# Edge items of a sparse graph layer in another order, with the last panels' own rows and the last features in tiles of their own

## The chip, the cores and the metric

One core of a Trainium2 chip runs the whole kernel. The metric is the time of one execution on the device in microseconds (us); of the kernel before, three executions took 3121.13 us (median), 3118.40 and 3138.08 us. One further execution was taken with the profiler on.

## The reference

The input x holds 32 graphs of 512 nodes with 256 features; one 512x512 adjacency matrix serves all. Four layers follow each other, of which the first and the last (called 0 and 3 in the names) have the same form:

```python
def _L0_gnn_ref(h_t, A_a, A_m, W1, b1, W2, b2, Wa, ba, Wm, bm, beta1, beta2, beta3):
    d = h_t.shape[-1]
    pre_u = jnp.einsum('bud,dk->buk', h_t, W1[:d])
    pre_v = jnp.einsum('bvd,dk->bvk', h_t, W1[d:])
    hidden = jax.nn.relu(pre_u[:, :, None, :] + pre_v[:, None, :, :] + b1)
    S = jax.nn.sigmoid(jnp.einsum('buvk,ko->buvo', hidden, W2)[..., 0] + b2[0])
    a_t = jnp.einsum('buv,bud->bvd', S * A_a, h_t)
    m_t = jnp.einsum('uv,bud->bvd', A_m, h_t) * h_t
    return (beta1 * h_t + beta2 * (jnp.einsum('bvd,de->bve', a_t, Wa) + ba)
            + beta3 * (jnp.einsum('bvd,de->bve', m_t, Wm) + bm))
...
    x = _L0_gnn_ref(x, adj, adj, ...)   # layer 0; A_a and A_m are both adj
    x = _L1_gnn_ref(x, adj, ...)        # z + relu((adj z) W' + b)
    x = _L2_gnn_ref(x, adj, ...)        # dense attention: softmax(leaky_relu(f_i + f_j) + adj) feats + x
    x = _L3_gnn_ref(x, adj, adj, ...)
```

Only some ten entries in a row of adj are not zero, so S is needed only there.

## The kernel before, in words

**Groups.** The 32 graphs go in eight groups of NB = 4, numbered t = 0 to 7. A group passes four streams of work: `first` (pre-activations of layer 0 into a table in memory), `edges` of layer 0 (the values of S at the edges), `middle` (the sums of layer 0, layers 1 and 2, the pre-activations of layer 3) and `edges` and `last` of layer 3. `sparse_path` gives every piece of every stream a due time in units of one group's middle stage, and `weave` issues the pieces in the order of these times, so that pieces of neighbouring groups alternate on each engine. Every engine executes its own instructions in the order in which they stand in its queue.

**Items.** An edge item is a set of 128 edges of the graph, one for each partition, handled for the four graphs of the group at once. Each of the four blocks of 128 nodes has OWN = 8 items (one edge per node and item); edges beyond eight per node go to PANELS = 2 panel items for each half of the node range. That makes ITEMS = 36 in a pass of `edges`, and there are 16 passes (two in each group). Blocks 0 and 1 and their panels form the first half of S, blocks 2 and 3 the second.

**One item.** `fetch` gathers the rows of the far ends (`rows`, 512 KB, an indirect DMA on GpSimd's queue, line 607) and needs the near ends' rows (`mine`): for a block's items these are one contiguous tile, loaded once by SyncE (line 647) and shared by its eight items; for a panel they are gathered by a second indirect DMA on GpSimd (also through line 607). There are three buffers for `mine`. VectorE adds the two (line 686), multiplies the positive part by W2 (line 694 or 702), ScalarE or VectorE sums, and after each four items a sigmoid follows (exp in line 592, then lines 596, 597 and 636). `put` then scatters the item's 128x4 values into memory (`cells`, an indirect DMA on GpSimd, line 601). There is one `cells` tensor for each half of S; two puts into the same tensor are kept apart by a wait for the earlier one to land. So `put` takes from the list `ready` the first entry that belongs to the other half than the put before it, if there is one. Rows are fetched LEAD = 3 items ahead; in the first pass of the kernel (layer 0, t = 0) and in the last (layer 3, t = 7) it is LEAD_AT_ENDS = 5, with some more tiles for rows (`rows_more`).

**S in use.** `load` reads the filled half tensors back as four tiles `SA` of 1 MB (line 727, GpSimd's queue); tiles 0 and 1 come from the first half, 2 and 3 from the second. In `middle` ScalarE copies one graph out of each (`flat`, line 809), and TensorE multiplies (line 840); in layer 3 TensorE reads SA itself (line 1001).

**The end.** For t = 7 the work of layer 3 that does not need S is done ahead by `last_before`: for each of four graphs it loads the features x2 (`h`, line 957, two buffers) and their transpose (`hT`, line 962, one buffer), and TensorE makes hWa and mhT from them (line 45; copies in lines 740 and 750) and keeps them in tiles `big`. `last_behind` then loads SA and does the sums (lines 1001, 1010, 1013) and the store (line 985).

**The order of the items** is a list made once for all passes; `h0` and `h1` below are the halves:

```python
order = [item_of(0, j) for j in range(OWN // 2)]
for lead, other in ((0, 2), (2, 1), (1, 3)):
    for j in range(OWN // 2):
        order += [item_of(lead, OWN // 2 + j), item_of(other, j)]
tail = [panel_of(h, q) for h in range(2) for q in range(PANELS)]
for j in range(OWN // 2):
    order.append(item_of(3, OWN // 2 + j))
    order += tail[j : j + 1]
```

By halves this reads 0000, then twelve pairs that alternate, then 1 0 1 0 1 1 1 1: the last eight are block 3's second four items with the panels h0, h0, h1, h1 between them.

Of the kernel before, what the change touches and what calls it, by code (L numbers as in the profile page):

```python
# [8 lines left out]
F32 = mybir.dt.float32  # L9
# [7 lines left out]
P = 128  # L17
N = 512
D = 256
NC = N // P  # L20
DC = D // P
# [7 lines left out]
OWN = 8  # L29
PANELS = 2  # L30
LINES = PANELS * P
LEAD = 3
LEAD_AT_ENDS = 5
TAIL = 6
CELLS = HALF * N
ITEMS = NC * OWN + 2 * PANELS
SPARE = NC // 2 * OWN * P + LINES
GROUP = NB * D
# [173 lines left out]
def item_of(c, k):  # L212
    return c * OWN + k


def panel_of(half, q):
    return NC * OWN + half * PANELS + q


class Edges:  # L220
# [3 lines left out]
    def __init__(self, m, pool):  # L224
        nc = self.nc = m.nc
        self.m = m
        self.iu = pool.tile([P, 2 * PANELS], I32, name="iu")
        self.iv, self.cell = (pool.tile([P, ITEMS], I32, name=n) for n in ("iv", "cell"))
        self.value = pool.tile([P, ITEMS], F32, name="value")
        self.inode = pool.tile([P, 2 * PANELS], I32, name="inode")  # L230

        order = [item_of(0, j) for j in range(OWN // 2)]
        for lead, other in ((0, 2), (2, 1), (1, 3)):
            for j in range(OWN // 2):
                order += [item_of(lead, OWN // 2 + j), item_of(other, j)]
        tail = [panel_of(h, q) for h in range(2) for q in range(PANELS)]
        for j in range(OWN // 2):
            order.append(item_of(3, OWN // 2 + j))
            order += tail[j : j + 1]
        self.order = order  # L240

    def value_of(self, j):
# [172 lines left out]
class Sparse:  # L415
# [192 lines left out]
            out=rows, out_offset=None, in_=g.table, in_offset=bass.IndirectOffsetOnAxis(ap=at, axis=0)  # L608
        )

    def edges(self, g, spare=()):

        nc, e, w = self.nc, self.e, g.w
        flat = "p c b -> p (c b)"
        own = g.self_s.rearrange(flat)
        ready, fetched = [], {}
        lead = LEAD_AT_ENDS if spare else LEAD
        tags = [None] * 5 + list(spare)  # L620
        mine = {}
        places = g.table.rearrange("(c p k) n -> c k p n", p=P, k=2)

        def own_1():
            self.sigmoid_of(own)
            diag = self.counts.diag.unsqueeze(2).to_broadcast([P, NC, NB])
            nc.vector.tensor_tensor(g.self_s, g.self_s, diag, ALU.mult)
            for q in range(2):
                diagonal = g.cells[q][q * HALF : q * HALF + HALF * (N + 1), :]
                diagonal = diagonal.rearrange("(c p a) b -> p c a b", p=P, a=N + 1)[:, :, 0, :]  # L630
                nc.sync.dma_start(diagonal, g.self_s[:, 2 * q : 2 * q + 2, :])

        def run_1(ks):
            self.sigmoid_of(g.s[:, ks, :].rearrange(flat))
            value = e.value[:, ks].unsqueeze(2).to_broadcast([P, ks.stop - ks.start, NB])
            nc.vector.tensor_tensor(g.s[:, ks, :], g.s[:, ks, :], value, ALU.mult)
            for k in range(ks.start, ks.stop):
                j = e.order[k]
                ready.append((e.half_of(j), e.cell[:, j : j + 1], g.s[:, k, :]))

        def fetch(n):
            j = e.order[n]
            c = j // OWN
            if c >= NC or c not in mine:
                t = self.gath.tile([P, GROUP], F32, name="mine", bufs=3)
                if c < NC:
                    nc.sync.dma_start(t, places[c, 0])
                    mine[c] = t
                else:
                    self.fetch(t, g, e.iu[:, j - NC * OWN : j - NC * OWN + 1])  # L650
            else:
                t = mine[c]
            if tag := tags[n % len(tags)]:
                rows = self.act.tile([P, GROUP], F32, name="rows_more", tag=tag)
            else:
                rows = self.gath.tile([P, GROUP], F32, name="rows")
            self.fetch(rows, g, e.iv[:, j : j + 1])
            fetched[n] = rows, t

        def put():  # L660

            at = next((n for n, r in enumerate(ready) if r[0] != self.half), 0)
            if ready:
                r = ready.pop(at)
                self.half = r[0]
                self.put(g, *r)

        def sums(k, rows):

            for b in range(NB):  # L670
                part = rows[:, b * D : (b + 1) * D]
                self.behind(nc.scalar.activation(part, part, AF.Identity, accum_out=g.s[:, k, b : b + 1]))  # L672

        summed = []
        self.half = 1
        for n in range(lead):
            fetch(n)
            yield

        todo = [(2, lambda: self.exp_of(w, own)), (4, own_1)]  # L680
        done = 0
        for k in range(ITEMS):
            for _ in range(2 if spare and len(ready) > 2 else 1):
                put()
            rows, other = fetched.pop(k)
            self.behind(nc.vector.tensor_tensor(rows, rows, other, ALU.add))  # L686
            if k + lead < ITEMS:
                fetch(k + lead)
            if summed:
                summed.pop(0)()  # L690
            if spare or k % 2 == 1 and k < ITEMS - 3:
                by_entry = rows.rearrange("p (b d) -> p b d", b=NB)
                w2 = w["W2bc"].unsqueeze(1).to_broadcast([P, NB, D])
                nc.vector.scalar_tensor_tensor(by_entry, by_entry, 0.0, w2, ALU.max, ALU.mult)  # L694
                summed.append(lambda k=k, rows=rows: sums(k, rows))
                if spare:
                    summed.pop(0)()
            else:
                for b in range(NB):
                    part = rows[:, b * D : (b + 1) * D]  # L700
                    at = g.s[:, k, b : b + 1]
                    nc.vector.scalar_tensor_tensor(part, part, 0.0, w["W2bc"], ALU.max, ALU.mult, accum_out=at)  # L702
            if k % 4 == 3 or k >= ITEMS - 3:
                ks = slice(done, k + 1)
                near = spare or k >= ITEMS - 5
                todo.append((k + (1 if near else 3), lambda ks=ks: self.exp_of(w, g.s[:, ks, :].rearrange(flat))))
                todo.append((k + (1 if near else 4), lambda ks=ks: run_1(ks)))
                done = k + 1
            while todo and todo[0][0] <= k:
                todo.pop(0)[1]()  # L710
            yield
        for _, f in todo:
            f()
        for _ in range(TAIL - 1):
            put()
            yield
        while ready:
            put()
        yield
# [237 lines left out]
        self.nc.sync.dma_start(h, self.x2s[i])  # L957
        return h

    def x2T_of(self, i):  # L960
        hT = self.act.tile([P, DC, N], F32, name="hT3", tag="hT")
        self.nc.sync.dma_start(hT, self.x2T[i])
        return hT

    def last_before(self, g, i):

        self.ends = []
        for b in range(NB):
            h, hT = self.x2_of(i + b), self.x2T_of(i + b)
            both = self.big(F32, 2048, 0).rearrange("p (k n) -> p k n", k=2)  # L970
            hWa = both[:, 0, :].rearrange("p (c d) -> p c d", c=NC)
            mhT = both[:, 1, :].rearrange("p (c n) -> p c n", c=DC)
            for _ in self.hWa(g, hT, 3, hWa):
                yield
            for _ in self.mhT(h, hT, 3, mhT):
                yield
            self.ends.append((hWa, mhT))
# [78 lines left out]
def edge_times(ahead, a, b, behind, lead=LEAD):  # L1056

    step = (b - a) / ITEMS
    first = [ahead + j * min(step, (a - ahead) / lead) for j in range(lead)]
    return first + spread(even(ITEMS), a, b) + spread(even(TAIL), b, behind)  # L1060
# [18 lines left out]
def sparse_path(ctx, m, counts, xr, outr, B):  # L1079


    sp = Sparse(ctx, m, counts, xr, outr, B)
    last = B // NB - 1
# [6 lines left out]
    for t in range(last + 1):  # L1090
        g0, g3 = Group(sp, m.g0, f"0_{t}"), Group(sp, m.g3, f"3_{t}")
# [11 lines left out]
        edges3 = edge_times(end + 0.003, end + 0.05, end + 0.48, end + 0.54)  # L1103
        behind = end + 0.56, end + 1.13
        if t == last - 1:
            edges3 = edge_times(end + 0.003, end + 0.05, end + 0.46, end + 0.5)
            behind = end + 0.7, end + 1.06
        if t == last:
            end -= 0.2
            edges3 = edge_times(end + 0.003, end + 0.02, end + 0.45, end + 0.46, LEAD_AT_ENDS)  # L1110
# [2 lines left out]
            (sp.first(g0, t * NB), first, "fill"),  # L1113
            (sp.edges(g0, ("yT", "mhT3") if t == 0 else ()), edges0, ""),
            (sp.middle(g0, g3, t * NB), spread(middle_shares(t == 0), start, end), "main"),
            (sp.edges(g3, ("yT", "h1", "hT1") if t == last else ()), edges3, "free"),
        ]
        if t == 0:
            streams.append((sp.middle_before(g0, 0), spread(AHEAD, -0.15, -0.03), ""))
# [243 lines left out]
```

## Time and profile before

| what | us |
|---|---|
| median of three executions | 3121.13 |
| the profiled execution | 3102.14 |
| its span | 3100.4 |
| TensorE busy in the span | 2714.6 |
| VectorE busy | 2302.8 |
| GpSimd busy | 1522.5 |
| first four S tiles (SA of layer 0, t = 0): first and last load issued at | 242.9 and 262.1 |
| last pass of edges: first row gather and last put issued at | 2885.6 and 3039.3 |
| last S tiles: last load issued at | 3042.5 |
| last matmul group begins at | 3092.2 |

Times inside the span are counted from its start. One period, from a group's SA loads to the next group's, lasts some 358 us (1872 to 2230). Busy times of a stretch of the profile (columns: stretch, length, busy us and count of each engine, mean granted TensorE clock, share of the DMA engines, GB/s moved):

```profile
1877.00:2235.00 358.00, 333.61 (x1072) 202.84 (x1071) 281.91 (x764) 155.44 (x464) 187.98 (x160) 0.97 0.71 229
2880.00:3100.40 220.40, 161.88 (x566) 123.36 (x564) 115.84 (x154) 70.95 (x315) 99.33 (x80) 0.88 0.55 185
```

The engines stand in the order TensorE matmul, TensorE weight load, VectorE, ScalarE, GpSimd. In a period in the midst of the kernel TensorE is busy for 334 of 358 us; in the last 220 us it is busy for 162.

### The profile page before, as it was taken

How to read it: one execution, taken by the hardware profiler on the slowest of the kernel's cores; microseconds unless marked ns; L12 is line 12 of the kernel's file. 1: busy time of each engine (PE TensorE's matmuls, PEld its weight loads, DVE VectorE, ACT ScalarE, POOL GpSimd, SP SyncE). 2: the span in 40 equal slices, each digit the busy share in tenths (PEclk: the TensorE clock that was granted, in tenths of full speed). 3: DMA queues.
4: the chain of work that ended last, by engine and by line, in shares of the span. 5: the costliest groups of instructions: out<-in, count | busy, mean ns of one | idle time of the engine just before them, and what ended most of it. 6: DMA issues, size and time to landing. Idle time of an engine off the chain costs nothing.

```text
span 3100.4 us, 32465 instructions
## 1 busy us (share of the span) xinstructions
PE 2714.6 (88%) x8645; PEld 1642.5 (53%) x8646; DVE 2302.8 (74%) x6026; ACT 1337.8 (43%) x4101; POOL 1522.5 (49%) x1312
## 2 busy tenths in 40 slices
PE   6366888889998999989998999989999899889957
PEld 3133444446654565546664565545664566545636
DVE  6783886889589875989589885888679795772761
ACT  3453554445345433545354442545335343453440
POOL 1462453556346563556346562565436563450561
PEclk9688988999999999999999999999999999999978
DMA  8874556786677766786668766787568766551753
GB/s 285 282 236 152 180 174 225 237 268 213 223 224 263 235 210 219 247 282 213 227 213 258 238 197 213 242 267 237 188 216 268 251 221 208 178 174 58 234 195 115
DMA packets 302719, 679.40 MB, mean 219 GB/s; under 512 B 52672, under 2 KB 170944, under 8 KB 294336
## 3 DMA queue, kind: packets, MB, share of 16 engines
q0 software_dynamic: 120384, 406.01, 41.0%
q1 hardware_dynamic: 163184, 234.01, 22.5%
q10 hardware_dynamic: 18960, 37.24, 3.2%
q8 instruction: 70, 1.15, 0.2%
q14 instruction: 121, 0.99, 0.1%
HBM read 531.12 MB, written 146.01 MB: 218 GB/s over the span
## 4 chain that ended last, share of the span: by engine, by line
PE 51%; DVE 18%; DMA 17%; issue 6%; ACT 4%; POOL 3%; SPq 0%; POOLq 0%; ACTq 0%; DVEq 0%
PE pst L45 24%; PE pst L1001 7%; DVE rows L686 6%; DMA table<-puv 5%; DMA rows<-table,iv 5%; PE pst L570 3%; DVE rows L702 3%; PE pst L861 3%; PE pst L1010 3%; PE pst L572 3%; DMA cells<-s,cell 3%; DVE rows L694 3%; PE pst L883 2%; PE pst L840 2%; DMA SA<-cells 2%
## 5 line engine op out<-in xcount | busy, mean ns | idle before, releaser
L601 POOL DMA_INDIRECT cells<-s,cell x576 | 691.1, 1200 | 740.7 <-DMA cells<-s,cell 370.3
L607 POOL DMA_INDIRECT rows<-table,iv x554 | 663.3, 1197 | 672.7 <-DMA table<-puv 148.1
L686 DVE TENSOR_TENSOR rows<-rows,mine 128x1024 f32<-128x1024 f32 x554 | 670.8, 1219 | 164.7 <-DMA rows<-table,iv 148.8
L672 ACT ACTIVATE rows<-rows 128x256 f32<-128x256 f32 x1096 | 442.9, 407 | 516.7 <-DVE rows L694 511.1
L45 PE MATMUL pst<-adj,h 128*128 128x512 f32 x1024 | 451.3, 592 | 0.3 <-PE pst L941 0.3
L702 DVE SCALAR_TENSOR_TENSOR rows<-rows,L_gnn_W2bc 128x256 f32<-128x256 f32 x1120 | 415.9, 419 | 1.8
L45 PE MATMUL pst<-L_gnn_Wa,hT 128*128 128x256 f32 x1024 | 264.3, 410 | 118.6 <-DMA hT<-xT 64.6
L694 DVE SCALAR_TENSOR_TENSOR rows<-rows,L_gnn_W2bc 128x1024 f32<-128x1024 f32 x274 | 332.3, 1216 | 0.3
L45 PEld LDWEIGHTS pst<-adj,h 128*128 128x128 f32 x1024 | 192.8, 190 | 222.4 <-issue 218.4
L45 PEld LDWEIGHTS pst<-L_gnn_Wa,hT 128*128 128x128 f32 x1024 | 207.7, 208 | 165.8 <-issue 53.1
L45 PE MATMUL pst<-eT,feats 128*128 128x512 f32 x512 | 231.5, 606 | 12.4 <-ACT eT L953 12.4
L45 PE MATMUL pst<-adjT,zW 128*128 128x512 f32 x512 | 227.8, 597 | 6.2 <-ACT zW L865 6.2
L1001 PEld LDWEIGHTS pst<-hWa,SA 128*128 128x128 f32 x896 | 213.7, 328 | 7.7 <-issue 4.5
L1001 PE MATMUL pst<-hWa,SA 128*128 128x256 f32 x896 | 216.8, 398 | 0.0
L861 PE MATMUL pst<-WT,hT 128*128 128x256 f32 x512 | 150.3, 459 | 75.9 <-DVE hT L848 75.9
L672 ACT ACTIVATION_READ_ACCUMULATOR rows<-rows 128x1 f32 x1096 | 206.7, 189 | 0.0
L809 ACT COPY flat<-SA 128x512 f32<-128x512 f32 x128 | 137.6, 1128 | 155.0 <-PE pst L45 60.1
L840 PE MATMUL pst<-flat,hWa 128*128 128x512 f32 x448 | 196.8, 592 | 0.0
L861 PEld LDWEIGHTS pst<-WT,hT 128*128 128x128 f32 x512 | 118.0, 235 | 114.9 <-DVE hT L848 88.1
L575 ACT COPY puv<-pst 128x256 f32<-128x256 f32 x256 | 93.7, 370 | 183.8 <-DVE puv L574 168.1
L574 DVE TENSOR_TENSOR puv<-pst,bc_L_gnn_b 128x256 f32<-128x256 f32 x256 | 105.0, 416 | 90.3 <-DMA table<-puv 53.8
L45 PEld LDWEIGHTS pst<-eT,feats 128*128 128x128 f32 x512 | 97.5, 193 | 127.5 <-issue 109.8
(170 smaller groups left out, 3979.3 us busy)
## 6 DMA issues: line engine op xcount, KB each, us to landing
table<-puv SPq DMA_DIRECT2D x256, 256.0 KB, 5.5
SA<-cells POOLq DMA_DIRECT2D x64, 1024.0 KB, 7.0
h<-in_x_dram SPq DMA_DIRECT2D x64, 512.0 KB, 6.4
mine<-table SPq DMA_DIRECT2D x64, 512.0 KB, 5.3
hT<-xT SPq DMA_DIRECT2D x36, 512.0 KB, 5.1
h<-x2s SPq DMA_DIRECT2D x36, 512.0 KB, 4.1
xT<-hT ACTq DMA_DIRECT2D x32, 512.0 KB, 5.5
x2T<-yT SPq DMA_DIRECT2D x32, 512.0 KB, 5.3
```

Of the source, the lines that this page charges most:

```text
L45: nc.tensor.matmul(out, lhsT, rhs, start=(n == 0), stop=(n == len(pairs) - 1))
L574: nc.vector.tensor_tensor(puv[:, 0, :], pp[:, 0:D], w["b1bc"], ALU.add)
L601: self.nc.gpsimd.indirect_dma_start(out=g.cells[half], out_offset=bass.IndirectOffsetOnAxis(ap=at, axis=0), in_=s, in_offset=None)
L607: self.nc.gpsimd.indirect_dma_start(out=rows, out_offset=None, in_=g.table, in_offset=bass.IndirectOffsetOnAxis(ap=at, axis=0))
L672: self.behind(nc.scalar.activation(part, part, AF.Identity, accum_out=g.s[:, k, b : b + 1]))
L686: self.behind(nc.vector.tensor_tensor(rows, rows, other, ALU.add))
L694: nc.vector.scalar_tensor_tensor(by_entry, by_entry, 0.0, w2, ALU.max, ALU.mult)
L702: nc.vector.scalar_tensor_tensor(part, part, 0.0, w["W2bc"], ALU.max, ALU.mult, accum_out=at)
L809: self.nc.scalar.copy(flat[:, r, :], SA[r][:, :, b])
L840: nc.tensor.matmul(pz, hWa[:, r, cs], flat[:, r, :], start=(r == 0), stop=False)
L861: nc.tensor.matmul(pw[:, at], zT[:, d, cs], m.WT_1[:, d, :], start=(d + k == 0), stop=(d * k == 1))
L1001: nc.tensor.matmul(pz[:, k * D : (k + 1) * D], SA[r][:, cs, b], hWa[:, r, :], start=(r + k == 0), stop=False)
```

## The change

It has three parts. The list of items gets another order, for all 16 passes: blocks 0 and 2 run together up to the end of block 2, then blocks 1 and 3; the panels of the second half come in between, at places 20 and 27, and those of the first half at places 33 and 35. By halves: 0 0, then 16 that alternate, then 0 1 1 0 1 0 1 0 1 1 0 1 0 1 (places 18 to 31), then 1 0 1 0. In the last pass alone, the four panels' own rows are gathered after the first few items into tiles `held`, whose memory belonged to `eT`, `hWa0` and `mhT0` of the middle stage. And in `last_before` the transposed features of the second to fourth graph get a tile of their own each, in the memory of the S tiles of layer 3.

```diff
-        order = [item_of(0, j) for j in range(OWN // 2)]
-        for lead, other in ((0, 2), (2, 1), (1, 3)):
-            for j in range(OWN // 2):
-                order += [item_of(lead, OWN // 2 + j), item_of(other, j)]
-        tail = [panel_of(h, q) for h in range(2) for q in range(PANELS)]
-        for j in range(OWN // 2):
-            order.append(item_of(3, OWN // 2 + j))
-            order += tail[j : j + 1]
+        ends, most = OWN // 4, OWN - OWN // 4
+        order = [item_of(0, j) for j in range(ends)]
+        for j in range(most):
+            order += [item_of(0, ends + j), item_of(2, j)]
+        for j in range(ends):
+            order += [item_of(1, j), item_of(2, most + j)]
+        for j in range(most):
+            order += [item_of(1, ends + j), item_of(3, j)]
+            if j % (most // PANELS) == 0:
+                order.append(panel_of(1, j // (most // PANELS)))
+        for j in range(ends):
+            order += [item_of(3, most + j), panel_of(0, j)]
...
-    def edges(self, g, spare=()):
+    def edges(self, g, spare=(), panels=()):
...
-            if c >= NC or c not in mine:
+            if j in held:
+                t = held.pop(j)
+            elif c >= NC or c not in mine:
...
+        def hold():
+
+            js = [j for j in e.order if j >= NC * OWN]
+            for tag in panels:
+                n = 2 if tag == "eT" else 1
+                t = self.act.tile([P, n, GROUP], F32, name="held", tag=tag)
+                for k in range(n):
+                    j = js.pop(0)
+                    held[j] = t[:, k, :]
+                    self.fetch(held[j], g, e.iu[:, j - NC * OWN : j - NC * OWN + 1])
...
         for k in range(ITEMS):
             for _ in range(2 if spare and len(ready) > 2 else 1):
                 put()
+            if k == LEAD_AT_ENDS:
+                hold()
...
-    def x2T_of(self, i):
-        hT = self.act.tile([P, DC, N], F32, name="hT3", tag="hT")
+    def x2T_of(self, i, hT=None):
+        if hT is None:
+            hT = self.act.tile([P, DC, N], F32, name="hT3", tag="hT")
...
-            h, hT = self.x2_of(i + b), self.x2T_of(i + b)
+            room = self.big(F32, 2048, 3)[:, 0 : DC * N].rearrange("p (c n) -> p c n", c=DC) if b else None
+            h, hT = self.x2_of(i + b), self.x2T_of(i + b, room)
...
-            (sp.edges(g3, ("yT", "h1", "hT1") if t == last else ()), edges3, "free"),
+            (sp.edges(g3, *((("yT", "h1", "hT1"), ("eT", "hWa0", "mhT0")) if t == last else ())), edges3, "free"),
```

More of the change, by code (lines that the diff above doesn't have):

```diff
@@ L230, in __init__ @@
         self.inode = pool.tile([P, 2 * PANELS], I32, name="inode")
-        order = [item_of(0, j) for j in range(OWN // 2)]
-        for lead, other in ((0, 2), (2, 1), (1, 3)):
-            for j in range(OWN // 2):
-                order += [item_of(lead, OWN // 2 + j), item_of(other, j)]
-        tail = [panel_of(h, q) for h in range(2) for q in range(PANELS)]
-        for j in range(OWN // 2):
-            order.append(item_of(3, OWN // 2 + j))
-            order += tail[j : j + 1]
+        ends, most = OWN // 4, OWN - OWN // 4
[10 more added lines that the diff above has]
+            order += [item_of(3, most + j), panel_of(0, j)]
+        assert len(order) == len(set(order)) == ITEMS
         self.order = order
@@ L620, in edges @@
         tags = [None] * 5 + list(spare)
-        mine = {}
+        mine, held = {}, {}
         places = g.table.rearrange("(c p k) n -> c k p n", p=P, k=2)
```

## The prediction

> **What bounds the kernel now.** I read the page's busy slices first, then the chain of waits in order of time, then the timelines of GpSimd, VectorE and TensorE at the places where the chain leaves TensorE. TensorE is busy for 88% of the span and for 334 of 358 us in a period of the middle, so there an order of items can win little. The two ends are different: in the last 220 us it is busy for 162. The end of the chain of waits (start us, us, what):
>
> ```profile
> 2985.86 5.36 DMA rows_more<-table,iv
> 3004.48 8.06 DMA mine<-table,iu
> 3024.31 4.51 DMA hT<-x2T
> 3028.96 12.12 PE pst L45 x32
> 3042.54 8.43 DMA SA<-cells
> 3051.02 8.57 PE pst L1001 x26
> ```
>
> It runs from row gathers to a panel's own rows, to a feature load that had to wait for its only buffer, and then to the S tiles. From 3051.0 on nothing but TensorE's sums remains (35.8 of the 40 us from 3060 are busy), so the span ends 49.4 us after the last S tile is there. GpSimd's timeline shows what holds that tile (start, us, engine, line, what, idle before and its releaser):
>
> ```profile
> 3002.94 1.24 POOL L607 DMA_INDIRECT rows<-table,iv  x1 [0.30 <-issue]
> 3004.48 0.94 POOL L607 DMA_INDIRECT mine<-table,iu  x1 [0.30 <-issue]
> 3005.72 0.94 POOL L607 DMA_INDIRECT mine<-table,iu  x1 [0.30 <-issue]
> 3006.97 0.99 POOL L601 DMA_INDIRECT cells<-s,cell  x1 [0.30 <-issue]
> ...
> 3014.44 1.32 POOL L601 DMA_INDIRECT cells<-s,cell  x1 [5.18 <-DMA cells<-s,cell]
> ...
> 3039.33 0.97 POOL L601 DMA_INDIRECT cells<-s,cell  x1 [3.02 <-DMA cells<-s,cell]
> 3041.98 1.14 POOL L727 DMA_DIRECT2D SA<-cells  x2 [1.68 <-PE pst L1001]
> ```
>
> After the last row gather twelve puts follow in 32 us, each held until the one before it in the same half has landed. Eight of the twelve go to the second half: at 3006.97, 3014.44, 3019.33, 3022.49, 3027.20, 3030.50, 3035.32 and 3039.33, seven gaps with a mean of 4.62 us. VectorE loses its time in the same stage to rows that come late:
>
> ```profile
> 2999.09 1.27 DVE L686 TENSOR_TENSOR rows_more<-rows_more,mine 128x1024 f32<-128x1024 f32 x1 [3.50 <-DMA mine<-table,iu]
> 3012.56 2.36 DVE L686 TENSOR_TENSOR rows<-rows,mine 128x1024 f32<-128x1024 f32 x2 [8.06 <-DMA mine<-table,iu]
> ```
>
> From 2894 to 3020 its idle gaps sum to 26 us: 11.6 for panels' own rows, 15 for far rows. But GpSimd has no gaps to give: between 2911.7 and 3002.9 it waits about 8 us, all for puts to land, and otherwise issues back to back. The first group's end looks the same, on GpSimd and then on TensorE:
>
> ```profile
> 254.72 1.00 POOL L601 DMA_INDIRECT cells<-s,cell  x1 [0.30 <-ACT big L740]
> ...
> 262.08 1.15 POOL L727 DMA_DIRECT2D SA<-cells  x2 [3.85 <-DMA cells<-s,cell]
> ```
>
> ```profile
> 268.22 7.06 PE L840 MATMUL pst<-flat,big 128*128 128x512 f32 x9 [12.71 <-ACT flat L809]
> ```
>
> **What the skill says.** The Trainium skill, "SBUF — State Buffer", section "Who interferes with whom", says that VectorE ops in a two-port mode shut GpSimd out of their shared port while it writes DMA descriptors, and that a tensor_tensor was not seen to stall such a DMA. Here VectorE ran without a gap from 2913 to 2943, mostly tensor_tensor and scalar_tensor_tensor on f32, and GpSimd's 14 indirect DMAs took 23.8 us, 1.7 each; at 3004 to 3008, with VectorE idle, they took 0.94 to 0.99. I go by the trace: a VectorE that waits less makes each GpSimd DMA slower, and part of the gain goes back. The skill, "DMA: Bandwidth & Descriptors", section "Anatomy of one DMA — SWDGE (gpsimd) path", puts some 2 us of fixed cost, mostly the receipt of the write, on every such DMA however small. The 2 KB puts agree in kind (last put to SA load: 2.65 us), but in a row they cost 4.62; I use the trace.
>
> **The change, part by part.**
>
> *Own rows ahead, last pass.* Four gathers (0.95 us and 0.3 of issue each, 5 us) move from 2963, 2994, 3004 and 3006 to behind the tenth row gather, about 2904. GpSimd idles there (3.59, 2.33 and 3.47 us before 2907, for row buffers), so the cost is near nothing; their 2 MB meet a busy DMA (share 0.73), covered because far rows then land about 11 us before use. Without that cover it costs up to 5 us. The gaps of 3.50 and 8.06 go; what is late next is the far row, whose place in GpSimd's queue moves little: ahead of the last row gather stand two own-row gathers less and, in the new program's order, one put more, so it starts about 1.3 us earlier, at 3001.6. Then no own-row gather follows and the tail of puts begins at 3002.9 instead of 3007.0.
>
> *Order, last pass.* Of the twelve puts of the tail seven go to the second half instead of eight: six gaps of 4.62 us, last put at 3002.9 + 27.7 = 3030.6, so 8.7 us earlier. They need not wait for data: the last rows land at about 3007.6, and the before's 6.3 us from add to sigmoid's end put the last value at 3014. But the price: the before loads the first two S tiles at 3028.7 and 3033.3, between the puts; now the first half's panels are among the last puts, and all four loads stand behind them. In the before two loads came in at +6.6 and +9.0 us, so 2.5 for one more. The first goes out at 3031.6: the fourth lands at 3031.6 + 6.6 + 3 x 2.5 = 3045.7, against 3051.0. **Gain 5.3, I say 6**, since without the two late own-row gathers the first gap (7.47) should be shorter. Bounds: gaps of 3.9 give 10, gaps of 5.5 give 0; nothing forbids a small loss.
>
> *Own tiles for features.* The three loads go out together when the S tiles of t = 6 are free (their last matmuls end at 2949); TensorE then does its 4 x 10.5 us ahead by some 2995 instead of 3041, and no longer sits on the edge's path. By itself worth nothing while the S tiles come at 3045; it would have been next (3041) had they come earlier. SyncE: an output store and loads of h stand behind these three, 1 us of issue and no wait beyond 2949; the store itself waited until 2956. The S loads reuse these tiles, whose last reader, VectorE's product for the fourth graph, is done near 3003.
>
> *Order, first group.* After its last own-row gather (223.1) seven puts go to the second half, at 224.8 to 254.7, gaps of 5.0 us; after the change six: the last at 249.8. Four loads from 252.5 on arrive at +5.0 and then 2.5 each, as the two at 262.1 did: 265 against 269.5. **Gain 4.5, I say 5** (0 to 9); the panels' values exist later than nodes' (their gathers are at 138 to 142, their product waits 16 us), but places 20 and 27 come after those.
>
> *Order, the fourteen other passes.* At a layer-0 end the last put is bound by its data (value at 2222.5, put at 2227.7 behind three of its half). Now alternating, it goes at 2223; the loads follow from 2225 and the fourth lands at 2225.1 + 6.4 + 3 x 2.7 = 2239.6, when the before's did (2240.3). ScalarE waits in its queue on them, and VectorE and TensorE behind it:
>
> ```profile
> 2240.26 1.11 ACT L809 COPY flat<-SA 128x512 f32<-128x512 f32 x1 [2.63 <-DMA SA<-cells]
> ```
>
> ```profile
> 2242.24 1.97 PE L45 MATMUL pst<-L_gnn_Wa,hT 128*128 128x256 f32 x8 [0.97 <-DVE both L577]
> ```
>
> In the built program of later groups three of the `puv` copies now stand ahead of the last `flat`, so this 1 us goes in some of seven boundaries. At layer-3 ends earlier puts let the next group's rows start earlier; TensorE's only traces of that are two waits for `zW` (6.2 us in all). SyncE's load of block 3's rows moves behind up to four table writes in layer 3's passes; it lands near 1967 in the period from 1877, and its item is used after 1985. **Together 5** (-10 to +12).
>
> Sum: 6 + 5 + 5 = 16. The profiled execution takes 3102.1 (span 3100.4 and 1.7 around it), so 3086. The median shown lies 19 above it, at 3121; I take the gain from that: 3105.
>
> **Rivals.** *No difference* (within 6): the S loads behind one another eat what the puts give, at both ends; 3121. For it: four loads against two; against: five us less of puts at each end. *Much faster*: once the own rows are there, the far rows come in time too, VectorE runs through (26 us less), the first group gains its whole 12.7 us less one landing, and periods lose 1.5 us each: 22 + 8 + 8 = 38; 3083. Against it: GpSimd has no gaps, and slows when VectorE runs. *Slower*: the S loads at the layer-0 ends. If the last first-half put does not come earlier there, two loads more wait behind it, 2 x 2.5 us; `flat` holds ScalarE, so `puv`, the table writes and the first rows (2254.0) come 5 us later; VectorE waits in its queue for those (7.98 us at 2259.8 already) with the product that TensorE needs behind them. Seven boundaries and both ends at 5: +45, 3166; at half that, 3143. It decides where the last put gains less than two loads' time. Against it: the last values exist at 2222.5 and no longer wait for three landings. That the order does not alternate in fact is excluded by the built program.
>
> **Numbers.** About 1% (31 us) is what a measurement of this kernel can tell from no change, its three runs spread over 20 us. Forecast (gain of 8 to 26) 0.48; no difference 0.25; much faster 0.15; slower 0.12. Of these, the big case passes 31 us mostly, the forecast seldom: faster by over 1% 0.17; of the slower case half is over 31 us: 0.07; within 1% 0.76. The range runs from much faster (3082) to a mild form of slower (3136), 8 in 10.
>
> **What would show it.** Right: last put near 3030 less what the start gained, the four S loads within 3 us of each other, first full sum near 3045, no wait for `mine` after 2990, TensorE's hWa and mhT done before 3000; TensorE's wait for `flat` at 268 down from 12.7 to about 8. Wrong: VectorE still waits for panels' rows; gaps between puts of one half above 5.5 us; waits of TensorE for L577 or L848 longer at the boundaries; or a period that changes by more than 2 us.

## The result, and the profile after

The changed kernel takes 3156.09 us (median of 16 executions, 3141 to 3174) beside 3129.84 us of the kernel before on the same chip (16 executions, 3116 to 3138). The ratio is 1.0092 with a 95% interval of 1.0077 to 1.0107: slower by 26 us between the medians and by 29 us by the ratio, where 16 us of gain were forecast.

The two ends first. The chain of waits of the changed kernel (start us, us, what) now ends so:

```profile
3110.75 0.97 DMA cells<-s,cell
3111.72 6.05 DMA SA<-cells
3117.78 0.14 issue
3117.91 14.10 PE pst L1024 x54
...
3163.13 0.69 DVE h L1036
```

Neither a panel's own rows nor a feature load stands in it any more: puts, S tiles, sums. GpSimd's timeline at that place, from the last row gather to the loads:

```profile
3087.97 0.96 POOL L612 DMA_INDIRECT rows<-table,iv  x1 [0.30 <-ACT rows L691]
...
3110.75 0.97 POOL L606 DMA_INDIRECT cells<-s,cell  x1 [2.07 <-DMA cells<-s,cell]
3111.72 1.16 POOL L748 DMA_DIRECT2D SA<-cells  x2
3113.37 1.05 POOL L748 DMA_DIRECT2D SA<-cells  x2 [0.49 <-issue]
```

The twelve puts after the last row gather (3088.0) are through after 22.8 us (before: from the last gather of own rows, 3005.7, to 3039.3, 33.6 us), and the four loads go out within 2.2 us of each other. TensorE's timeline shows that it is done with its work ahead long before:

```profile
261.02 2.08 PE L861 MATMUL pst<-flat,big 128*128 128x512 f32 x2 [6.82 <-ACT flat L830]
...
3117.91 2.49 PE L1024 MATMUL pst<-big,SA 128*128 128x256 f32 x5 [36.70 <-DMA SA<-cells]
```

At the first group's end its longest wait for `flat` is 6.8 instead of 12.7 us. All of this was forecast in kind. The loss must lie between, in the fourteen other passes.

**A second pair of profiles.** The profiled execution of before (3102) was quicker than nearly all executions of that kernel, the one of the changed kernel (3169) slower than most of its own, so that their difference of 67 us is more than twice that of the medians. Both kernels were profiled once more, at 3117.66 and 3150.11 us; that pair, 32 us apart, is the one compared from here on. TensorE's waits in it, before and then after (engine, line, what it waited for: us in total, times, longest):

```profile
PE pst L861 <- DVE hT L848: 101.3, 21, 11.5
PE pst L45 <- DMA hT<-xT: 73.1, 4, 35.7
PE pst L45 <- DMA hT<-x2T: 43.7, 4, 18.3
PE pst L952 <- DVE cols L912: 37.7, 6, 8.8
PE pst L952 <- DVE ex L913: 31.3, 23, 3.3
```

```profile
PE pst L882 <- DVE hT L869: 91.3, 22, 12.3
PE pst L45 <- DMA hT<-xT: 71.8, 4, 34.3
PE pst L973 <- DVE cols L933: 40.7, 7, 10.2
PE pst L1024 <- DMA SA<-cells: 36.9, 1, 36.9
PE pst L973 <- DVE ex L934: 32.5, 24, 3.3
PE pst L868 <- DVE mhT L771: 23.7, 5, 5.4
PE pst L577 <- DVE yT L951: 18.3, 6, 3.3
```

(Line 861 of before is 882 after, 952 is 973, and so on.) The waits of the middle are alike but for two that are new: for `mhT` and for `yT` at line 577, eleven waits and 42 us. At the end the waits for features fell from 43.7 to 2.7 us, and those for S tiles rose from 7.1 to 36.9. Counted by the start of each graph's sums, the changed kernel loses 53 us from the second graph to the last and gains 19 after that; up to the second graph it gains 1.

Waits are not the whole of the 53 us. These two lines give the stretch from the second graph's sums to the last's, before and then after (columns as in the profile before); 7352 matmuls begin in it in both (the counts take in some at its edges):

```profile
319.40:2832.70 2513.30, 2304.08 (x7355) 1378.05 (x7354) 1961.81 (x5316) 1111.17 (x3273) 1296.32 (x1110) 0.96 0.70 223
318.40:2884.50 2566.10, 2317.12 (x7354) 1375.12 (x7353) 1960.22 (x5316) 1110.70 (x3273) 1302.16 (x1110) 0.96 0.69 218
```

TensorE's idle time grows by 40 us and its busy time by 13. The longer busy time stands next to the new waits: the matmuls on `mhT` and on `yT` of this stretch are busy for 198.6 and 359.2 us instead of 186.3 and 350.5, and other matmuls for less.

**What VectorE is late for.** Both waits are for a product that stands in VectorE's queue behind an edge item, and that item waits for a panel's own rows. GpSimd, VectorE and TensorE of the changed kernel (second profile) around one of them:

```profile
927.52 0.98 POOL L612 DMA_INDIRECT rows<-table,iv  x1 [0.30 <-DVE both L583]
928.80 0.96 POOL L612 DMA_INDIRECT mine<-table,iu  x1 [0.30 <-issue]
...
937.61 0.93 POOL L612 DMA_INDIRECT mine<-table,iu  x1 [4.83 <-DVE rows L707]
```

```profile
931.46 0.69 DVE L771 TENSOR_TENSOR mhT<-pst,hT 128x512 f32<-128x512 f32 x1
936.12 1.22 DVE L707 TENSOR_TENSOR rows<-rows,mine 128x1024 f32<-128x1024 f32 x1 [3.65 <-DMA mine<-table,iu]
937.60 2.40 DVE L707 TENSOR_TENSOR rows<-rows,mine 128x1024 f32<-128x1024 f32 x2
942.52 0.68 DVE L771 TENSOR_TENSOR mhT<-pst,hT 128x512 f32<-128x512 f32 x1
```

```profile
943.25 4.42 PE L868 MATMUL pst<-mhT,L_gnn_Wm 128*128 128x512 f32 x6 [3.63 <-DVE mhT L771]
```

The own rows are gathered at 928.80 and used at 936.12. VectorE idles for them with two other items ready behind (they follow at once, at 937.60), the second `mhT` product comes late, and TensorE waits 3.6 us for it. GpSimd loses 4.8 us too: its next own-row gather needs the same tile. VectorE's wait happens once in each of twelve of the fourteen ordinary passes, always for the panel at place 20 and never for the one at 27; in five of the twelve, as here, VectorE's queue even has the panel's item ahead of those of places 18 and 19.

Why so late? In the new order blocks 1 and 3 run together, and each keeps one of the three `mine` tiles (places 14 to 30 and 19 to 34). The panels have only the third, and that is block 2's until the product of place 17. That product ran at 922.6 here; the gather of place 20 could not start before it was over, at 923.8. It left 5.0 us later still, behind a row gather, a put and another row gather in GpSimd's queue; in the twelve passes with the wait this second delay is 3.4 to 6.0 us. In the kernel before no panel stands within three places behind the item that frees its tile.

### The profile page after: what moved, and what is told of

Same layout as the page of the kernel before. It is cut to its first block, busy times and chain, and to the rows that moved or that the text cites. A ratio compares the mean times of both kernels' runs of the same rounds, so it can differ in the third digit from the quotient of the medians.

```text
span 3167.7 us, 32487 instructions
## 1 busy us (share of the span) xinstructions
PE 2726.1 (86%) x8645; PEld 1638.4 (52%) x8646; DVE 2301.6 (73%) x6026; ACT 1337.8 (42%) x4101; POOL 1526.9 (48%) x1312
## 5 line engine op out<-in xcount | busy, mean ns | idle before, releaser
L606 POOL DMA_INDIRECT cells<-s,cell x576 | 701.5, 1218 | 701.4 <-DMA cells<-s,cell 278.2
L45 PE MATMUL pst<-L_gnn_Wa,hT 128*128 128x256 f32 x976 | 247.7, 405 | 71.1 <-DMA hT<-xT 34.2
L45 PEld LDWEIGHTS pst<-L_gnn_Wa,hT 128*128 128x128 f32 x976 | 195.0, 205 | 113.4 <-DVE big L393 34.7
L882 PE MATMUL pst<-WT,hT 128*128 128x256 f32 x512 | 143.3, 442 | 97.8 <-DVE hT L869 97.8
L45 PEld LDWEIGHTS pst<-adjT,zW 128*128 128x128 f32 x512 | 97.2, 192 | 128.8 <-issue 109.5
```

The lines of the kernel that those rows point to most:

```text
L45: nc.tensor.matmul(out, lhsT, rhs, start=(n == 0), stop=(n == len(pairs) - 1))
L606: self.nc.gpsimd.indirect_dma_start(out=g.cells[half], out_offset=bass.IndirectOffsetOnAxis(ap=at, axis=0), in_=s, in_offset=None)
L882: nc.tensor.matmul(pw[:, at], zT[:, d, cs], m.WT_1[:, d, :], start=(d + k == 0), stop=(d * k == 1))
```

## The experiments

"Loss" below is against the kernel before, whose median was 3128 to 3131 us beside these kernels. The table gives what the traces show from 580 to 2760 us: VectorE's waits for panels' own rows, TensorE's waits for `mhT` and `yT` behind them, for `hT` at line 861/882, and in all. A slower kernel has done less of its work by 2760 us, so the last column makes its waits look somewhat short. Rows with a time in brackets are second profiles, of one execution each.

| kernel | median us | ratio to before | own rows | mhT + yT | hT | TensorE, all |
|---|---|---|---|---|---|---|
| before, second profile | (3117.66) | | 2.8 | 0.3 | 92.2 | 160.9 |
| changed, second profile | (3150.11) | | 50.7 | 42.1 | 85.6 | 189.8 |
| e1_order | 3167.26 | 1.0116 (1.0088 to 1.0144) | 52.5 | 42.7 | 83.9 | 191.2 |
| e2_ends | 3111.50 | 0.9945 (0.9926 to 0.9965) | 5.2 | 0.2 | 98.0 | 171.5 |
| e3_panels | 3108.49 | 0.9924 (0.9896 to 0.9952) | 0.0 | 1.0 | 97.2 | 166.9 |
| e4_spread | 3121.88 | 0.9960 (0.9944 to 0.9976) | 57.4 | 43.6 | 45.6 | 163.7 |
| e5_both | 3072.58 | 0.9813 (0.9776 to 0.9849) | 0.0 | 0.8 | 44.8 | 133.5 |
| e6_bunch | 3158.87 | 1.0092 (1.0070 to 1.0114) | 4.8 | 1.0 | 138.4 | 197.7 |
| e7_mid | 3132.25 | 1.0003 (0.9987 to 1.0019) | 0.5 | 0.0 | 79.6 | 170.5 |
| e8_ends_spread | 3118.38 | 0.9962 (0.9944 to 0.9980) | 5.3 | 0.0 | 52.0 | 153.3 |
| e11_tail | 3111.73 | 0.9947 (0.9930 to 0.9963) | 30.8 | 1.0 | 109.4 | 179.1 |
| e13_later | 3119.59 | 0.9975 (0.9961 to 0.9989) | 7.9 | 0.6 | 102.4 | 174.2 |
| e14_later_spread | 3095.53 | 0.9885 (0.9867 to 0.9904) | 7.0 | 0.8 | 71.9 | 155.8 |

**Which part of the change loses: e1_order and e2_ends.** The first has the new order alone, the second the old order with the last pass's two parts.

```diff
 # e1_order: the changed kernel, with these two undone
-            (sp.edges(g3, *((("yT", "h1", "hT1"), ("eT", "hWa0", "mhT0")) if t == last else ())), edges3, "free"),
+            (sp.edges(g3, ("yT", "h1", "hT1") if t == last else ()), edges3, "free"),
...
-            h, hT = self.x2_of(i + b), self.x2T_of(i + b, room)
+            h, hT = self.x2_of(i + b), self.x2T_of(i + b)
```

> The new order alone; the last pass gathers its panels' own rows in turn and has one tile for features, as before the change. Theory (T): the order costs the fourteen other passes about 40 us (waits of VectorE for rows behind the four bunched S loads at layer-3 ends, and for panels' own rows at places 20 and 27), and the parts in the last pass give back some 10 to 15. Then this kernel is slower than the changed one: about 3160 us (3150 to 3172) where before is 3130, with the same waits for hT at the layer-3 ends (about 60 us in sum). Rival (R): the loss sits in the last pass's parts (early gathers, tiles of their own), the order costs nothing: about 3130, waits for hT as before.

> The order of before; only the last pass's panels' own rows ahead and its features in tiles of their own. T: the fourteen other passes are those of before (sum of the waits for hT in layer-3 ends near 36 us, of those for panels' own rows near 13), the end gains a few us: 3115 to 3127, best guess 3122. R: these parts make the loss: 3150 or more.

Measured: 3167 and 3112. The order makes the loss, 36 us; the last pass's parts gain 20 with the old order (17 by the ratio) and 11 with the new. Theory T holds on that. The parts gain more than was expected of them: 3112 lies below the range of 3115 to 3127. And one thing in T doesn't hold: the expectation speaks of "places 20 and 27", and only 20 waits.

**Own rows of panels: e3_panels.** A tile of their own and an earlier gather; to make room, the pool of the small `s` tiles has one set instead of two.

```diff
+        def own_early(n):
+            if not spare and n < ITEMS - 1 and e.order[n] >= NC * OWN:
+                t = early[n] = self.gath.tile([P, GROUP], F32, name="own", bufs=1)
+                at = e.order[n] - NC * OWN
+                self.fetch(t, g, e.iu[:, at : at + 1])
...
+            own_early(k + 6)
             if k + lead < ITEMS:
                 fetch(k + lead)
```

> The changed kernel, but in all passes except the last and the first group's the own rows of a panel go to a tile of their own and are gathered six places ahead instead of three. T: the waits for panels' own rows (53 us over the passes in the changed kernel) fall under 10, TensorE's waits for the products queued behind them (mhT 25 us, yT 19 us) fall by about 30, and the time falls by half of the loss of the passes: about 3140 (3133 to 3148). Rival (R2): these waits lie beside other work of TensorE, or the late rows take their place; the bunched loads make the whole loss: 3156 (3150 to 3162).

Measured: 3108, 48 us below the changed kernel. VectorE's only remaining wait of this kind in the whole kernel (same columns as the waits above):

```profile
DVE rows L717 <- DMA mine<-table,iu: 0.8, 1, 0.8
```

The waits for `mhT` and `yT` fell by 41 us, and the time by somewhat more: from the second graph's sums to the last's, the matmuls on these tiles are back at 186.7 and 352.1 us of busy time, and all of TensorE's busy time is 9 us shorter than in the changed kernel's second profile. The guess of 3140 (3133 to 3148) was a miss on the timid side: it had put half of the loss down to the S loads.

**The S loads of layer 3: e4_spread, e6_bunch, e8_ends_spread.** After the change the four loads of a layer-3 end go out one behind the other. In the first profile of the changed kernel (GpSimd, VectorE, TensorE):

```profile
1038.34 1.17 POOL L748 DMA_DIRECT2D SA<-cells  x2
1040.11 0.53 POOL L748 DMA_DIRECT2D SA<-cells  x1 [0.60 <-DMA cells<-s,cell]
1040.95 1.14 POOL L612 DMA_INDIRECT rows<-table,iv  x1 [0.30 <-issue]
1042.40 1.61 POOL L612 DMA_INDIRECT rows<-table,iv  x1 [0.31 <-DVE self_s L602]
1044.00 0.58 POOL L748 DMA_DIRECT2D SA<-cells  x1
```

```profile
1052.86 1.23 DVE L707 TENSOR_TENSOR rows<-rows,mine 128x1024 f32<-128x1024 f32 x1 [9.62 <-DMA rows<-table,iv]
```

```profile
1054.74 1.65 PE L882 MATMUL pst<-WT,hT 128*128 128x256 f32 x3 [13.93 <-DVE hT L869]
```

Rows gathered at 1040.95, behind 3 MB of loads, are there 11.9 us later; own-row gathers, also of 512 KB, landed after 5.7 to 8.5 in the second profile (900 to 1300 us). The Trainium skill, "DMA: Bandwidth & Descriptors", section "Two DMAs through the same engine are not ordered", says that descriptors of one queue of a DMA engine start in order, though they are pipelined; GpSimd's gathers and loads share one queue in the profile (q0), and the 11.9 us agree with gathers that start behind the loads. In e4_spread each load goes behind a row gather of the next group:

```diff
+            if self.loads_due:
+                self.loads_due.pop(0)()       # in edges, after each fetch: one S load
...
+        self.tc.add_manual_dep(load.ins, self.gather, order, reason="behind the last row gather")
...
-        SA = self.load(g, 3)
+        SA = []
+        self.loads_due = [lambda: self.load_one(g, SA)] * NC
```

> The changed kernel, but the four S loads of layer 3 (all passes but the last) are given out one at a time, each behind a row gather of the next group. T: with the loads apart the rows land in time, TensorE's waits for hT at the layer-3 ends (62 us in sum over six ends in the changed kernel) fall to 30 or less, and the time falls by some 15 to 20: about 3139 (3131 to 3147). Rival (R3): the loads are not the cause, panels' own rows are: 3156 (3150 to 3162). A second way to fail: the loads come some 15 us later and the first sums wait for them, then waits for SA stand at the layer-3 sums.

Measured: 3122, 34 us off and below the expected range of 3131 to 3147. The waits of TensorE in e4_spread:

```profile
PE pst L897 <- DVE hT L884: 47.4, 21, 4.3
...
PE pst L883 <- DVE mhT L786: 24.8, 5, 5.7
PE pst L578 <- DVE yT L966: 18.8, 6, 3.7
```

`hT` is down from 91 to 47 us with none above 4.3, while the waits behind the panel at place 20 are untouched: two separate costs. But is this one the change's doing? Two runs ask for it.

```diff
 # e6_bunch: the kernel before; layer 3's loads in the order 2, 3, 0, 1, each behind the last
+        for c in (2, 3, 0, 1) if late else range(NC):
...
+                self.tc.add_manual_dep(ins.ins, names[-1], order, reason="behind the load before it")
```

> The kernel of before, but at layer 3 (all passes but the last) the S loads of the first half stand behind those of the second, so that all four go out one behind the other once the last put has landed, as in the changed kernel. If the bunching by itself costs TensorE time (M1), hT waits of the middle rise above 90 and the time by some 20 to 35: 3150 to 3165. If it does not (T2: the loss is all in the panels' own rows), 3130 (3122 to 3138).

> The order of before, the last pass's two parts, and layer 3's S loads given out one at a time. T2: the bunching of the loads is not the new order's doing (with the order of before the hT waits of the middle were 72 us in one profile and 98 in another, with the new order 84 to 97), so spreading helps this order as much: 3112 - 34 = 3078 (3068 to 3090), hT waits of the middle near 45. Rival (M1 as first stated: only the new order bunches the loads): no gain, 3108 to 3116.

Bunching the loads of the old order costs 28 us (3159), with `hT` waits of 138 us. So bunching has a price. Yet the changed kernel bunches, and its `hT` waits are no longer than before's (85.6 and 92.2): something else in the new order takes off about as much as the bunching adds. What that is was not found. And spreading the loads of the old order, which shortens its `hT` waits to 52, gained nothing: 3118 against 3112 of e2_ends, where 3078 was expected. A second profile of it,

> The order of before with the last pass's parts and the loads spread, a second look: the first was of its quickest run (3100 of 3100 to 3130). Near its median, 3118: if the spreading helps this order too, hT waits of the middle stay near 50 and the time that came instead stands in other waits of TensorE (zW or SA, above 30 us in sum); if it does not help, hT waits are back above 70.

at 3112.58, has 71.3 us of `hT` waits, and waits for `yT` in the products behind layer 1 (line 883) of 15.5 us instead of e2_ends' 4.8. Part of the gain is handed on there; the rest stays open.

**Second profiles.**

> The kernel of before a second time, unchanged: its first profile was taken of a run of 3102, among the quickest of its runs (3112 to 3147 in the last comparison). If that profile flattered the middle, this one, near 3130, has hT waits of the middle of 85 to 100 instead of 72, and hardly any waits for panels' own rows (under 10); if the hT waits are the new order's doing they stay near 72.

> The changed kernel a second time, unchanged, to have a profile nearer to its median of 3156: TensorE's waits for mhT and yT behind panels' own rows again near 44 us (40 to 48) if they come with the program; hT waits of the middle 80 to 100.

The `hT` waits of the unchanged kernel were 71.5 us in one profile and 92.2 in the other; the first profile had flattered it, and the idea that the new order lengthens these waits fell with that. The 42 us behind the panels came again.

**Both edits: e5_both.**

> The changed kernel with both edits: panels' own rows in a tile of their own and ahead, and layer 3's S loads given out one at a time behind row gathers. Alone they took 48 and 34 us off. Theory T2 (two separate waits of TensorE, 44 us behind panels' own rows and some 45 us of the hT waits): they add up, 3156 - 48 - 34 = 3074 (3066 to 3086). Rival: both cure the same lateness of VectorE, then no more than the larger: 3100 to 3108.

Measured: 3073. The two costs add up, and this is the fastest kernel of the study, 1.9% below the kernel before.

**Is it the place of the panels? e7_mid and e11_tail.**

```diff
 # e7_mid: the kernel before, and
+        for place, j in ((20, panel_of(1, 0)), (27, panel_of(1, 1))):
+            order.remove(j)
+            order.insert(place, j)
 # e11_tail: the changed kernel, and the same with places 29 and 31
```

> The kernel of before with nothing changed but the places of two panels of the second half: 20 and 27 instead of the tail, as in the new order. T2: that alone makes the loss: waits for panels' own rows near 50 us, TensorE's waits for mhT and yT behind them near 44, time 3131 + 40 = 3171 (3158 to 3178). Rival (the taking of turns makes the loss, the panels' places matter only together with it): 3131 (3125 to 3140).

> The changed kernel with the two panels of the second half moved back from places 20 and 27 to 28 and 31; the taking of turns, the buffers and the last pass's parts stay. T2: the waits for panels' own rows inside the graphs' matmuls go, as with a tile of their own: 3112 (3104 to 3124); in the last pass the puts of the second half bunch again at the end, which may give back up to 5. Rival (the extra tile, not the places, made the gain of e3): 3150 to 3160.

e7_mid is a miss, and the most telling one: 3132, no loss, no wait. Expected were 3158 to 3178. GpSimd in e7_mid issues the own-row gather of place 20 here, and VectorE uses it at 928 to 931:

```profile
882.20 1.04 POOL L610 DMA_INDIRECT mine<-table,iu  x1 [0.30 <-issue]
```

More than 45 us ahead: in this order block 0 gives its tile back at place 10, so that the tile of place 20 is long free. LEAD is 3 in both kernels, but in GpSimd's queue this gather stands behind 14 of the pass's row gathers here and behind 22 in the changed kernel. The place alone costs nothing; it needs the new order's hold on the tiles. e11_tail takes the panel away from place 20 (to 28) and is at 3112 with no extra tile. VectorE still waits 31 us for own rows, in every second pass at place 31, but TensorE's waits for `mhT` and `yT` behind them are 1 us. There, too, products for TensorE stand behind the waiting item, as VectorE's and TensorE's lines around one such wait show:

```profile
1130.35 1.23 DVE L710 TENSOR_TENSOR rows<-rows,mine 128x1024 f32<-128x1024 f32 x1 [5.33 <-DMA mine<-table,iu]
1138.15 0.69 DVE L896 TENSOR_TENSOR yT<-yT,hT 128x512 f32<-128x512 f32 x1
```

```profile
1136.21 3.62 PE L1036 MATMUL pst<-L_gnn_Wm,mhT 128*128 128x256 f32 x16
1139.66 3.63 PE L907 MATMUL pst<-WT,yT 128*128 128x257 f32 x16
```

TensorE has other matmuls until 1139.66, and `yT` is ready by then. The same wait of VectorE costs TensorE time only where the product behind it is needed next.

**The distance alone: e13_later and e14_later_spread.** One constant moves the two panels from 20 and 27 to 22 and 29, five places behind the product that frees the tile instead of three.

```diff
-            if j % (most // PANELS) == 0:
+            if j % (most // PANELS) == 1:
```

> The changed kernel with the second half's panels two places later, 22 and 29 instead of 20 and 27; nothing else differs. In the traces every wait for a panel's own rows in the ordinary passes belongs to the panel at place 20, whose tile comes free with the product of place 17. If the short way from 17 to 20 is the cause (T3), two places more take the waits away: mhT and yT waits behind them under 6 us, time as with the extra tile, 3110 (3102 to 3120). If any panel between the blocks' items costs the time, or the extra tile or the earlier gather were needed, 3140 to 3160.

> The same, and layer 3's S loads given out one at a time behind row gathers: without an extra tile it should do what the two edits did together before, 3075 (3064 to 3088), against 3130 for the kernel before the change. If the extra tile was part of that, 3095 to 3115.

Measured: 3120, and no such wait of TensorE is left. In e13_later the gather goes out behind the same product,

```profile
922.50 0.98 POOL L612 DMA_INDIRECT mine<-table,iu  x1 [0.30 <-issue]
```

8.5 us after it (914.0), and the item is used at 933.1: 10.6 us later, where the changed kernel had 7.3 and a wait in them. The tile is free at 915.2, and the gather leaves 7.3 us behind that, later than in the changed kernel: what has grown is the time left for the rows to land. The distance is the cause for 37 us of the 48 that e3_panels gained; the extra tile is worth the remaining 11, as it is worth 23 in e5_both against e14_later_spread (3096: the range of 3064 to 3088 was missed, the one named for the case that the extra tile has a part was met). In that second pair the `hT` waits differ by 27 us (71.9 and 44.8); why they do, and where the 11 come from, stays open.

## Why the prediction was wrong, step by step

**The order, the fourteen other passes** ("together 5 (-10 to +12)"): this step failed. It weighed the layer-0 ends, the layer-3 ends and SyncE's load of block 3's rows, and put the own rows of the two panels that the new order moves into the middle of these passes at nothing, without a reason. It knew how the first and the last pass wait for such rows, and the three buffers stood in its description of the kernel; that two of them are held from place 19 to 30 and the third comes free at 17 was not worked out. Measured, in the matched pair: 53 us lost from the second graph to the last, of which 42 are TensorE's waits behind place 20 and 13 its longer busy time (21 more on the matmuls of `mhT` and `yT`, 8 less elsewhere), while its other waits are 2 us shorter in sum; 36 to 48 us by medians (e1_order against before, the changed kernel against e3_panels). Without that wait the order is worth nothing either way: e3_panels, e11_tail and e13_later lie 3 us below, on, and 8 us above e2_ends.

**Order, last pass, and own tiles for features** (6 together): the first part was right, the size was not. From the start of the last graph's sums in layer 0 to the last row gather the matched pair gains 4.2 us (forecast 4.1), the puts gain 11.8 (forecast 4.6), and from the last put to the end it gains 3.4 (forecast: 3.4 lost to the bunched loads). Together 19 instead of 5.3. The gain forecast for the rows ahead and the tiles, nothing but what the order lets through, was too small as well: without the order the two together gain some 17 to 20 us in e2_ends (they were not run apart). That the tiles would be the next limit once the S tiles come earlier was right; in e1_order the last put is followed by 65 us to the end, against 57 in the changed kernel, and TensorE still has matmuls for hWa and mhT to do when the S loads are already out.

**Order, first group** (5): the wait for `flat` shrank from 13.5 to about 8 us in the second pair, but by the second graph's sums only 1 us of it is left. The arithmetic of the loads was right: ScalarE copies the fourth S tile at 265.40 instead of 270.05, 4.7 us earlier. What was left out is that the four tiles now come one by one: TensorE waits four times, 10.7 us in all instead of 13.5, and the ten matmuls behind its last wait start 2.2 us earlier (266.54 instead of 268.74) but take 7.2 us instead of 6.0.

**The rivals.** *Slower* had the right side and the wrong place. Its price was to come from `flat` at the layer-0 ends; ScalarE's waits for S tiles did grow, from 63 to 88 us, but TensorE waited for `flat` only at the first group's end. Its waits for `zW`, another product of ScalarE, grew from 1.3 to 9.1 us; without those for `mhT` and `yT` all its waits from the second graph's sums to the last's are 206 us against 208 before. Two of the signs named as proof of an error did appear: VectorE waits for panels' rows, in twelve passes, and the period changed by more than 2 us: it grew by 9 us (five periods together from 1782 to 1827 us), 7 of them the waits for `mhT` and `yT`. The other two signs that concern the middle did not: in the second pair TensorE's waits for L577 (now line 582) fell from 6.9 to 3.2 us and those for L848 (now 869) from 101.3 to 91.3.

## What to carry to other kernels

When an order of work is changed, write down for each buffer which item frees it and how many items later the next user needs its data; a prefetch distance is only as long as that, whatever the constant says. A wait of a helper engine costs what stands behind it in its queue and is needed next: 31 us of the same wait cost TensorE 1 us of waiting at one place, and 51 us cost it 42 at another. And one profile of a kernel whose executions spread by 1% can show a whole group of waits 20 us too short: before a difference between two profiles is explained, see how each stands to its own median.

## What the runs showed of the hardware that was not expected

A 512 KB row gather on GpSimd's queue, issued behind three 1 MB loads on the same queue, took 11.9 us to be usable, and four loads in a row made the median landing of an S tile 10.0 us (7.2 before). The price of bunching was found in both orders (28 us put in by e6_bunch, 34 taken out by e4_spread), but taking it out gained nothing in the old order. The same matmuls of TensorE were busy for longer where it had to wait in between: 198.6 us instead of 186.3 for those on `mhT`. And 57 executions of the unchanged kernel on one chip spread from 3112 to 3147 us.
